# Third sweep of a four-layer graph kernel: the product with the attention weights as seven products of quarters, over pairs of row tiles

## The chip, the cores and the metric

One Trainium2 chip, of which the kernel uses one core. The time is that of one execution on the device, in microseconds (us); the number quoted for a kernel is the median of its runs.

## The reference

Four layers over a graph of 2708 nodes with 512 features, each followed by a residual and a layer norm. `adj` is dense in storage (2708 x 2708). The change lies in layer 1, the attention layer:

```python
h = x @ W_sa
s_left = h @ a_sa[0, :Hd]
s_right = h @ a_sa[0, Hd:]
e = where(adj != 0, exp(-leaky_relu(s_left[:, None] + s_right[None, :], 0.01)), 0)
attn = e / (sum(e, axis=1, keepdims=True) + 1e-05)
x_a = attn @ h
x_b = adj @ (x @ W_gcnb) + b_gcnb
return sigmoid(attn_a * x_a + attn_b * x_b)      # attn_a, attn_b: gates per row
...
x = layernorm(x + layer1(x))
```

The kernel computes `attn @ (x @ W_sa)` as `(e @ x) @ W_sa`, with the row's share `attn_a / (sum(e) + 1e-05)` as a factor behind it.

## The kernel before

The work is a row of seven sweeps over the adjacency matrix; one each for layer 0, the graph convolution and the attention of layer 1, the three hops of layer 2, and layer 3. The change is in the third (index 2, line 1207, `sweep(S[2], RANGES, ...)`).

**Halves and ranges.** The nodes are split into a lower half (h=0) and an upper half (h=1) of 1354 nodes. A sweep takes output columns in ranges: for this sweep (0, 384), (384, 384), (768, 256), (1024, 330), each for both halves at once. With two halves of rows, two of columns and two halves of the features, a range is a product of 2x2 blocks, which the kernel does as seven products P1 to P7 (Strassen's scheme in Winograd's form): s1 to s4 are sums of adjacency blocks, made by VectorE (`comb`, line 411), T1 to T4 sums of feature blocks. Each of P1 to P7 is 10 steps of two 128 x (range's width) matmuls (`step`, line 473), into PSUM banks u, c, d and a, two of each. P1 fills u, P7 c, P5 d; P6 goes on into u, P4 into c, P3 into d, and P2 fills a. Of the eight banks six are so held from P5 to P4.

**Attention weights in this sweep.** Adjacency blocks 11, 21, 22 and 12 are loaded by SP (`load`, line 394). Before a block is used, ScalarE makes `e` from the row of scores (lines 1136 and 1137, a leaky relu and an exponential), and VectorE puts it where the adjacency isn't zero (line 1138). Adjacency tiles, s3 and `e` come from one ring of 38 buffers (`ring_tile`, `trans`), as do sums of finished rows (`d7`).

**What follows a range** (`done2`, line 1158). For each half a range leaves a transposed result C[h, 0..3] of 128 features x width. For each row tile of 128: fetch XB (the gated graph convolution) on SP; multiply with W_sa (`dense`, line 642: eight matmuls of 128x256, W[2] being eight tiles of 128 x 256 in spare parts of the feature tiles); scale with the row's share and add XB on VectorE (line 1170); sigmoid on ScalarE (1173); fetch X1, add, layer norm (1176 to 1179); store X2; transpose on PE and store X2T (1183, 1187); multiply with the last hop's weights W[3] (1191), copy on ScalarE (1193), store Y0. The upper half of a range follows from position 5.15 of its 7 on, the lower half from 7.12 on, in the next range's first positions.

**Order.** Every piece of work is put on a list with a position, in units of one of P1 to P7 (`at`, line 177); `S[2]` is where the third sweep begins. The list, sorted, is the order of priority for a scheduler that places each instruction on its engine when by its own model inputs and buffers are there: an instruction that isn't ready is overtaken by later ones. Those put on the list with `hold` get an extra edge to the instruction before them on their engine (the loop at the end of the program), so they overtake nothing. Each engine then runs its instructions in the order so fixed, waiting where it must.

**Buffers that matter here:** `nat` (6 of 128x512, for fetched tiles and y0), `tmp` (17, for C and rows of scores), `ring` (38), and the eight banks.

**Seven products over pairs of tiles** exist already for the second sweep (`done1`, line 1104 to 1118) and the seventh (`done6`). A pair is the row tile at the same place in both halves. `weight_sums` (655) makes T1 to T4 of the weight's quarters, `row_sums` (666) S1 to S4 of both halves' C, S1 in place and S2 to S4 in six ring tiles; `seven` (680) does six matmuls of 128x256 in a first part and eight in a second, in two banks shared by homes u, c and d, a, and adds what each holds into the output tiles on VectorE, nine times with a scale, with three of the nine behind the first part.

Of the kernel before, what the change touches and what calls it, by code (L numbers as in the profile page):

```python
# [21 lines left out]
F32 = mybir.dt.float32  # L22
BF = mybir.dt.bfloat16
AF = mybir.ActivationFunctionType
ALU = mybir.AluOpType
P = 128
EPS = 1e-5
NH = 1354
KT = 11
# [39 lines left out]
def gnn_kernel(ctx: ExitStack, tc: tile.TileContext, x, adjT, w_sa, a_sa, w_gcn, b_gcn, wab, bab, w_hop, w_out,  # L69
# [76 lines left out]
    def move(queue, dst, src):  # L146

        m = dst.shape[0]
        c = m - m % 16 if m > 16 else m
        queue.dma_start(out=dst[:c], in_=src[:c])  # L150
        if c < m:
            queue.dma_start(out=dst[c:m], in_=src[c:m])

    def ring_tile(nm):
        return pool.tile([P, 384], F32, name=nm, tag="ring", bufs=RING)
# [21 lines left out]
    def at(pos, fn, hold=False):  # L177

        def go():
            n = len(nc.cur_bb.bb.instructions)  # L180
            fn()
            held.update(range(n, len(nc.cur_bb.bb.instructions)))

        events.append((pos, len(events), go if hold else fn))

# [21 lines left out]
    def spare_part(s, g):  # L207

        return groups[s, g][0][:, 2, :]
# [383 lines left out]
    def layernorm(dsts, y, w, on_scalar=False, late=None):  # L593
        st = small.tile([P, 6], F32, name="st")
        nc.vector.bn_stats(st[:w], y[:w])
        mv = small.tile([P, 2], F32, name="mv")
        nc.vector.bn_aggr(mv[:w], st[:w])
        rstd = small.tile([P, 2], F32, name="rstd")
        nc.vector.tensor_scalar(rstd[:w, 0:1], mv[:w, 1:2], EPS, None, ALU.add)  # L599
        nc.gpsimd.tensor_tensor(rstd[:w, 1:2], rstd[:w, 0:1], neg_half[:w], ALU.pow)  # L600
        if on_scalar:
            nc.vector.scalar_tensor_tensor(rstd[:w, 0:1], mv[:w, 0:1], -1.0, rstd[:w, 1:2], ALU.mult, ALU.mult)
        for d, c0, c1 in dsts:
            if on_scalar:
                fn = lambda d=d, c0=c0, c1=c1: nc.scalar.activation(d[:w], y[:w, c0:c1], AF.Identity,
                                                                    bias=rstd[:w, 0:1], scale=rstd[:w, 1:2])
                fn() if late is None else late.append(fn)
                continue
            nc.vector.tensor_scalar(d[:w], y[:w, c0:c1], mv[:w, 0:1], rstd[:w, 1:2], ALU.subtract, ALU.mult)
# [45 lines left out]
    def weight_sums(wq, homes):  # L655

        wt_ = {(f"T{i + 1}", c): homes[2 * i + c] for i in range(4) for c in range(2)}
        sub = lambda o, a, b: nc.vector.tensor_tensor(o, a, b, ALU.subtract)
        for c in range(2):
            sub(wt_["T1", c], wq(0, 1, c), wq(0, 0, c))  # L660
            sub(wt_["T3", c], wq(1, 1, c), wq(0, 1, c))
            sub(wt_["T2", c], wq(1, 1, c), wt_["T1", c])
            sub(wt_["T4", c], wq(1, 0, c), wt_["T2", c])
        return lambda v, c: wt_[v, c] if isinstance(v, str) else wq(*v, c)

    def row_sums(A, n):

        Y = {("A11", c): A[0, c] for c in range(2)}
        Y.update({("A12", c): A[0, 2 + c] for c in range(2)})
        Y.update({("A22", c): A[1, 2 + c] for c in range(2)})  # L670
        for c in range(2):
            for m, a, b, op in (("S3", A[0, c], A[1, c], ALU.subtract), ("S1", A[1, c], A[1, 2 + c], ALU.add),
                                ("S2", None, A[0, c], ALU.subtract), ("S4", A[0, 2 + c], None, ALU.subtract)):
                Y[m, c] = A[1, c] if m == "S1" else ring_tile("d7")
                a = Y["S1", c] if a is None else a
                b = Y["S2", c] if b is None else b
                nc.vector.tensor_tensor(Y[m, c][:, :n], a[:, :n], b[:, :n], op)
        return Y

    def seven(part, Y, wop, H, lo, w, outs, scales, bases):  # L680

        if part == 0:
            x, y = bank("ps_7"), bank("ps_7")
            H.update(u=x[:, :HD], c=x[:, HD:], d=y[:, :HD], a=y[:, HD:])
        for home, a, v in SEV[part]:
            for c in range(2):
                nc.tensor.matmul(H[home][:w], Y[a, c][:, lo : lo + w], wop(v, c),  # L687
                                 start=part == 0 and home in "ud" and c == 0, stop=c == 1, skip_group_check=True)

        def acc(i, e, home, first=False):  # L690
            o = outs[i][:w, e * HD : (e + 1) * HD]
            b = bases[i][:w, e * HD : (e + 1) * HD] if first else o
            if scales is None:
                nc.vector.tensor_tensor(o, H[home][:w], b, ALU.add)
            else:
                nc.vector.scalar_tensor_tensor(o, H[home][:w], scales[i], b, ALU.mult, ALU.add)

        if part == 0 and scales is None:

            nc.scalar.copy(outs[0][:w, :HD], H["u"][:w])  # L700
            nc.scalar.copy(outs[1][:w, HD:], H["c"][:w])
            acc(1, 1, "d")
        elif part == 0:
            acc(0, 0, "u", True)
            acc(1, 1, "c", True)
            acc(1, 1, "d")
        else:
            acc(0, 0, "a")
            for i, e in ((1, 1), (0, 1), (1, 0)):
                acc(i, e, "u", (i, e) != (1, 1))  # L710
            acc(1, 0, "c")
            acc(0, 1, "d")
            for i in range(2) if scales is None else ():
                e = slice(i * HD, (i + 1) * HD)
                nc.vector.tensor_tensor(outs[i][:w, e], outs[i][:w, e], bases[i][:w, e], ALU.add)

    def fetch(src, nm="ld"):
        t = nat(nm)
        move(nc.sync, t[: src.shape[0]], src)
        return t  # L720

    def store_T(dst, xT):
        nc.gpsimd.dma_start(out=dst.rearrange("(c p) i -> p c i", p=P), in_=xT)
# [404 lines left out]

    at(S[2] + 3.2, start2b)

    def prep2(R0, n, h, t, w, a):

        e = trans("e")
        nc.scalar.activation(e[:w, :n], row[R0, h][:w, :n], AF.Prelu, bias=s_right[:w, t : t + 1], alpha=0.01)  # L1136
        nc.scalar.activation(e[:w, :n], e[:w, :n], AF.Exp, scale=-1.0)  # L1137
        nc.vector.scalar_tensor_tensor(a[:w, :n], a[:w, :n], 0.0, e[:w, :n], ALU.not_equal, ALU.mult)  # L1138

    def extra2(pb, r, R0, n, A):  # L1140
# [14 lines left out]
        at(pb + 5.2, lambda: run_sums(R0, n, 0, share))  # L1155
        at(pb + 4.7, lambda: run_sums(R0, n, 1, share))

    def done2(p0, dp, last, R0, n, h, C, tiles):
        gots = []
        for i, (t, lo, w) in enumerate(tiles):  # L1160
            got = {}
            gots.append(got)

            def a(t=t, got=got):
                got["xb"] = fetch(XB[t])

            def b(t=t, lo=lo, w=w, got=got):
                px = dense(lambda c: C[h, c][:, lo : lo + w], W[2], w)
                y = got["xb"]
                nc.vector.scalar_tensor_tensor(y[:w], px[:w], rd[t][:w], y[:w], ALU.mult, ALU.add)  # L1170

            def c(t=t, w=w, got=got):
                nc.scalar.activation(got["xb"][:w], got["xb"][:w], AF.Sigmoid)

            def d(t=t, w=w, got=got):
                got["x1"] = fetch(X1[t])
                y = got["x1"]
                nc.vector.tensor_tensor(y[:w], y[:w], got["xb"][:w], ALU.add)
                layernorm([(y, 0, D)], y, w)
                move(nc.gpsimd, X2[t], y[:w])  # L1180

            def e(lo=lo, w=w, got=got):
                xT = transposed([(got["x1"], 0, D)], w)
                for g, (i0, m) in enumerate(RANGES2):
                    c0, c1 = max(R0 + lo, i0), min(R0 + lo + w, i0 + 2 * m)
                    if c0 < c1:
                        store_T(X2T[g, h][:, c0 - i0 : c1 - i0], xT[:, :, c0 - R0 - lo : c1 - R0 - lo])
                got["xT"] = xT

            def f(t=t, w=w, got=got):  # L1190
                ps = dense(lambda c: got["xT"][:, c, :w], W[3], w)
                o = nat("y0")
                nc.scalar.copy(o[:w], ps[:w])
                move(nc.gpsimd, Y0[t], o[:w])

            m = len(tiles)
            g = min(dp, 0.28)
            p = p0 + g * i
            q = p0 + g * m + 0.02 + 0.04 * i
            at(p - 0.3, a)  # L1200
            at(p, b)
            at(q, c)
            at(q + 0.1, d)
            at(q + 0.32 + 0.6 * dp * i, e)
            at(q + 0.5 + 0.6 * dp * i, f)
# [465 lines left out]
```

## Time and profile before

| | us |
|---|---|
| median of 3 runs | 2844.57 (2844.51 to 2844.64) |
| profiled execution | 2845.67 |
| its span, first to last instruction | 2843.9 |
| PE busy | 2810.6 |
| VectorE busy | 2200.2 |
| ScalarE busy | 541.3 |
| stretch around the third sweep: from before its first product to its last with the attention weights | 785 to 1352 |

The page of the profile gives the share of each engine, then forty slices of the span, the DMA queues, the chain of work that ended last, and the costliest groups of instructions: line, engine, operation, output and inputs by the program's names (buffer numbers left out), count, busy time, mean of one, and what the engine waited for before them. A 128x256 product in 32-bit floats shows as two PE passes. In the third sweep the four ranges' first products begin at about 834, 967, 1110 and 1215 us.

### The profile page before, as it was taken

The page shows a single profiled execution, that of the slowest core. Times are in us where ns is not written, and L with a number is a line of the kernel's source. Part 1 is how long each engine was busy: PE and PEld are TensorE (multiplying, and loading weights), DVE is VectorE, ACT ScalarE, POOL GpSimd, SP SyncE. Part 2 cuts the span into 40 slices and gives each one's busy share as a digit, 9 for nine tenths or more (in the row PEclk, how much of TensorE's full clock was granted, in tenths as well). Part 3 has the DMA queues.
Part 4 walks back from the last instruction along what each step waited for, and adds up shares of the span by engine and source line. Part 5 has one row for each costly group of instructions (what it writes and reads, how often), then busy time and mean ns, then how long its engine had stood idle before and what let it go on. Part 6 is the DMA issues. An engine that isn't in the chain of part 4 may idle for free.

```text
span 2843.9 us, 38510 instructions
## 1 busy us (share of the span) xinstructions
PE 2810.6 (99%) x11486; PEld 1927.0 (68%) x11486; DVE 2200.2 (77%) x5694; ACT 541.3 (19%) x1112; POOL 618.9 (22%) x1114
## 2 busy tenths in 40 slices
PE   7999999999999999999999999999999999999998
PEld 6899765658755656766666666666666666666665
DVE  6999699668736464654699778897888878899987
ACT  4644100101155454540100000000000100100001
POOL 0223232214310101123113033030330211601202
PEclk9999999999999999999999999999999999999999
DMA  7765476436534333564668667566675666854542
GB/s 236 243 193 181 144 229 216 153 126 195 189 92 141 108 116 104 179 193 146 201 207 249 198 208 234 163 210 203 197 234 173 189 194 181 242 167 146 178 141 91
DMA packets 369712, 511.17 MB, mean 180 GB/s; under 512 B 63568, under 2 KB 322884, under 8 KB 369504
## 3 DMA queue, kind: packets, MB, share of 16 engines
q1 hardware_dynamic: 303544, 371.61, 44.3%
q0 software_dynamic: 49376, 126.39, 13.2%
q10 hardware_dynamic: 16584, 10.71, 1.3%
q8 instruction: 91, 1.49, 0.2%
q14 instruction: 117, 0.96, 0.1%
HBM read 424.82 MB, written 83.66 MB: 179 GB/s over the span
## 4 chain that ended last, share of the span: by engine, by line
PE 89%; DVE 6%; issue 2%; DMA 1%; SPq 1%; ACT 1%; POOL 1%; POOLq 0%; DVEq 0%; ACTq 0%
PE accu L1337 12%; PE accd L1337 12%; PE accc L1337 12%; PE accd L484 7%; PE accu L484 7%; PE accc L484 7%; PE ps_d L648 6%; PE acca L1337 6%; PE acca L484 4%; PE accr L1408 2%; PE ps L687 2%; PE accd L470 2%; PE accc L470 2%; PE accu L470 2%; PE acca L470 1%
## 5 line engine op out<-in xcount | busy, mean ns | idle before, releaser
L1282 DVE TENSOR_TENSOR z<-z 128x339 f32<-128x339 f32 (+1 forms) x966 | 455.8, 505 | 11.5 <-PE accu L1337 3.6
L1355 ACT COPY q<-accu 128x338 f32<-128x338 f32 (+1 forms) x84 | 34.6, 444 | 996.1 <-PE accu L1337 896.6
L600 POOL TENSOR_TENSOR rstd<-rstd,neg_half 128x1 f32<-128x1 f32 (+3 forms) x91 | 60.8, 668 | 730.6 <-DVE rstd L599 475.8
L1337 PE MATMUL accc<-s,t 128*128 128x338 f32 (+1 forms) x644 | 198.1, 450 | 0.0
L1337 PE MATMUL accd<-z,t 128*128 128x338 f32 (+1 forms) x644 | 193.9, 448 | 1.4 <-DVE q L1419 1.4
L1337 PE MATMUL accc<-z,t 128*128 128x338 f32 (+1 forms) x644 | 193.5, 448 | 0.6 <-ACT q L1355 0.6
L1337 PE MATMUL accu<-z,t 128*128 128x338 f32 (+1 forms) x644 | 193.8, 448 | 0.0
L1470 POOL DMA_DIRECT2D Y<-y x192 | 105.2, 554 | 364.0 <-DVE y L1465 330.8
L414 DVE TENSOR_TENSOR a<-a,a 128x384 f32<-128x384 f32 (+2 forms) x330 | 163.8, 512 | 23.2 <-PE accu L484 21.7
L1337 PEld LDWEIGHTS accc<-s,t 128*128 128x128 f32 x644 | 120.9, 190 | 64.1 <-issue 7.5
L1337 PEld LDWEIGHTS accc<-z,t 128*128 128x128 f32 x644 | 122.0, 190 | 61.6 <-issue 1.0
L1337 PEld LDWEIGHTS accd<-z,t 128*128 128x128 f32 x644 | 121.9, 190 | 61.2 <-DVE q L1419 2.1
L1337 PEld LDWEIGHTS accu<-z,t 128*128 128x128 f32 x644 | 121.8, 190 | 59.9 <-issue 0.5
L1282 DVE TENSOR_TENSOR s<-z 128x338 f32<-128x338 f32 (+1 forms) x322 | 150.3, 504 | 9.3 <-PE accc L1337 8.0
L1361 DVE TENSOR_TENSOR q<-q,accd 128x338 f32<-128x338 f32 (+1 forms) x112 | 56.2, 502 | 122.3 <-PE accd L1337 122.2
L1138 DVE SCALAR_TENSOR_TENSOR a<-a,e 128x384 f32<-128x384 f32 (+2 forms) x160 | 77.4, 507 | 44.4 <-ACT e L1137 38.6
L1136 ACT ACTIVATE e<-row,s_right 128x384 f32<-128x384 f32 (+5 forms) x176 | 96.4, 569 | 75.1 <-PE accc L484 19.2
L1034 DVE SCALAR_TENSOR_TENSOR mask<-a,mask 128x384 bf16<-128x384 f32 (+2 forms) x152 | 75.9, 506 | 12.5 <-DMA a<-in_adjT 11.2
L417 POOL DMA_DIRECT2D As<-a x120 | 64.9, 545 | 86.9 <-DVE a L414 65.1
L821 DVE SCALAR_TENSOR_TENSOR s<-a,row 128x384 f32<-128x384 f32 (+2 forms) x152 | 75.4, 507 | 7.4 <-ACT row L806 7.4
L1137 ACT ACTIVATE e<-e 128x384 f32<-128x384 f32 (+5 forms) x176 | 79.4, 477 | 1.9
L648 PE MATMUL ps_d<-w,xT 128*128 128x512 f32 (+1 forms) x176 | 79.2, 593 | 0.4 <-ACT xT L639 0.4
(742 smaller groups left out, 5884.8 us busy)
## 6 DMA issues: line engine op xcount, KB each, us to landing
z<-As SPq DMA_DIRECT2D x320, 169.5 KB
z<-As SPq DMA_DIRECT2D x320, 169.0 KB
a<-in_adjT SPq DMA_DIRECT2D x240, 192.0 KB
z<-in_adjT SPq DMA_DIRECT2D x240, 169.5 KB
z<-in_adjT SPq DMA_DIRECT2D x240, 169.0 KB
a<-in_adjT SPq DMA_DIRECT2D x120, 165.0 KB
a<-in_adjT SPq DMA_DIRECT2D x112, 128.0 KB
As<-a POOLq DMA_DIRECT2D x60, 192.0 KB, 3.3
```

Source lines behind the costliest of these rows:

```text
L414: nc.vector.tensor_tensor(A[r, dst, k][:, :n], A[r, a, k][:, :n], A[r, b, k][:, :n], op)
L470: nc.tensor.matmul(B[home, c][:, c0 : c0 + w], a[:, i * P : (i + 1) * P], x[:, d : d + w], start=bool(start and c0 == 0), stop=stop, skip_ ...
L484: nc.tensor.matmul(B[home, c][:, :n], X[STAT[p], k][:, c * P : (c + 1) * P], A[r, MOV[p], k][:, :n], start=bool(start and k == k0), stop=k ...
L648: nc.tensor.matmul(o, lhs(c), r, start=c == 0 and n == 0, stop=c == DC - 1, skip_group_check=True)
L821: nc.vector.scalar_tensor_tensor(t[:w, :n], a[:w, :n], 0.0, row[R0, h][:w, :n], ALU.is_gt, ALU.mult)
L1034: nc.vector.scalar_tensor_tensor(d[:w, :n], a[:w, :n], 0.0, d[:w, :n], ALU.not_equal, ALU.add)
L1136: nc.scalar.activation(e[:w, :n], row[R0, h][:w, :n], AF.Prelu, bias=s_right[:w, t : t + 1], alpha=0.01)
L1137: nc.scalar.activation(e[:w, :n], e[:w, :n], AF.Exp, scale=-1.0)
L1138: nc.vector.scalar_tensor_tensor(a[:w, :n], a[:w, :n], 0.0, e[:w, :n], ALU.not_equal, ALU.mult)
L1282: nc.vector.tensor_tensor(d[:, :n], Z[x + (k,)][:, :n], Z[y + (k,)][:, :n], op)
L1337: nc.tensor.matmul(B[home][:, :n], stat(v, k), a[:, :n], start=bool(start and k == 0), stop=k == nk - 1, skip_group_check=True)
L1470: nc.gpsimd.dma_start(out=rows[:, :, f * P : (f + 1) * P], in_=o[32 * f : 32 * (f + 1), : m * P].rearrange("p (b d) -> p b d", d=P))
```

## The change

In ranges one to three of the third sweep, the product with the attention weights is done for pairs of row tiles, by `seven`, after both halves of the range are there. `row_sums` makes the sums of both halves; `sums2` the sums of W_sa's quarters, with T1 and T2 in spare parts of B21 and B22, T3 in the place of quarter (0, 1) and T4 in the tile `vec`. The last range keeps the plain product, for which `again` loads quarter (0, 1) anew. Pairs follow each other by 1.0 position, from 7.62 of their range; the second part of `seven` comes 0.26 behind the first. `hold` can now be an engine: then only that engine's instructions of the piece are tied to the order of the list. So are the transposes and the product with W[3] of a pair, on PE. The function `node_sums`, which the diff also adds, is called nowhere and left out here.

```diff
--- before
+++ after
@@ -179,7 +179,9 @@
         def go():
             n = len(nc.cur_bb.bb.instructions)
             fn()
-            held.update(range(n, len(nc.cur_bb.bb.instructions)))
+            for i in range(n, len(nc.cur_bb.bb.instructions)):
+                if hold is True or nc.cur_bb.bb.instructions[i].engine == hold.engine:
+                    held.add(i)
 
         events.append((pos, len(events), go if hold else fn))
 
@@ -1128,6 +1130,20 @@
 
     at(S[2] + 3.2, start2b)
 
+    def sums2():
+        v = const.tile([P, D], F32, name="vec", tag="vec")
+        sa = lambda r, e, c: W[2][2 * (2 * r + c) + e]
+        t1, t2 = ([spare_part(s, g) for g in "BD"] for s in ("B21", "B22"))
+        W[9] = weight_sums(sa, t1 + t2 + [sa(0, 1, c) for c in range(2)] + [v[:, :HD], v[:, HD:]])
+
+    def again():
+
+        for c in range(2):
+            nc.scalar.dma_start(out=W[2][2 * c + 1], in_=w_sa[c * P : (c + 1) * P, HD:])
+
+    at(S[2] + 6.4, sums2)
+    at(S[2] + 23.4, again)
+
     def prep2(R0, n, h, t, w, a):
 
 
@@ -1155,11 +1171,77 @@
         at(pb + 5.2, lambda: run_sums(R0, n, 0, share))
         at(pb + 4.7, lambda: run_sums(R0, n, 1, share))
 
...
+    def pairs2(p0, R0, n, C, tiles):
+        Y = {}
+        at(p0 + 0.2, lambda: Y.update(row_sums({(i, c): C[1 - i, c] for i in range(2) for c in range(DC)}, n)))
+        for i, (t0, lo, w) in enumerate(tiles):
+            ts = (t0 + KT, t0)
+            xb, x1, xT, H = [], [], [], {}
+
+            def a(ts=ts, xb=xb):
+                xb.extend(fetch(XB[t]) for t in ts)
+
+            def b(part, ts=ts, lo=lo, w=w, xb=xb, H=H):
+                seven(part, Y, W[9], H, lo, w, xb, [rd[t][:w] for t in ts], xb)
+
+            def c(w=w, xb=xb):
+                for y in xb:
+                    nc.scalar.activation(y[:w], y[:w], AF.Sigmoid)
+
+            def d(ts=ts, x1=x1):
+                x1.extend(fetch(X1[t]) for t in ts)
+
+            def e(j, ts=ts, w=w, xb=xb, x1=x1):
+                y = x1[j]
+                nc.vector.tensor_tensor(y[:w], y[:w], xb[j][:w], ALU.add)
+                layernorm([(y, 0, D)], y, w)
+                move(nc.gpsimd, X2[ts[j]], y[:w])
+
+            def f(j, lo=lo, w=w, x1=x1, xT=xT):
+                v = transposed([(x1[j], 0, D)], w)
+                for g, (i0, m) in enumerate(RANGES2):
+                    c0, c1 = max(R0 + lo, i0), min(R0 + lo + w, i0 + 2 * m)
+                    if c0 < c1:
+                        store_T(X2T[g, 1 - j][:, c0 - i0 : c1 - i0], v[:, :, c0 - R0 - lo : c1 - R0 - lo])
+                xT.append(v)
+
+            def g(j, ts=ts, w=w, xT=xT):
+                ps = dense(lambda c: xT[j][:, c, :w], W[3], w)
+                o = nat("y0")
+                nc.scalar.copy(o[:w], ps[:w])
+                move(nc.gpsimd, Y0[ts[j]], o[:w])
+
+            p = p0 + 0.5 + 1.0 * i
+            at(p - 0.25, a)
+            at(p + 0.15, d)
+            for j in range(2):
+                at(p + 0.26 * j, lambda j=j, b=b: b(j))
+                at(p + 0.45 + 0.02 * j, lambda j=j, e=e: e(j))
+                at(p + 0.84 + 0.06 * j, lambda j=j, f=f: f(j), nc.tensor)
+                at(p + 1.22 + 0.22 * j, lambda j=j, g=g: g(j), nc.tensor)
+            at(p + 0.4, c)
+
     def done2(p0, dp, last, R0, n, h, C, tiles):
-        gots = []
+        if not last:
+            if h == 0:
+                pairs2(p0, R0, n, C, tiles)
+            return
         for i, (t, lo, w) in enumerate(tiles):
             got = {}
-            gots.append(got)
 
             def a(t=t, got=got):
                 got["xb"] = fetch(XB[t])
```

More of the change, by code (lines that the diff above doesn't have):

```diff
@@ L1156, in extra2, with node_sums @@
         at(pb + 4.7, lambda: run_sums(R0, n, 1, share))
+    def node_sums(x, y):
+        Z = {}
+        r = [ring_tile("d7").rearrange("p (c i) -> p c i", i=P)[:, :2, :] for _ in range(4)]
+        a, b = (v[:, i : i + 2, :] for v in (x, y) for i in (0, 2)), None
+        a11, a12, a21, a22 = a
+        for m, o, p, q, op in (("S3", r[0], a11, a21, ALU.subtract), ("S1", r[1], a21, a22, ALU.add),
+                               ("S2", r[2], r[1], a11, ALU.subtract), ("S4", r[3], a12, r[2], ALU.subtract)):
+            nc.vector.tensor_tensor(o, p, q, op)
+            Z.update({(m, c): o[:, c, :] for c in range(2)})
+        for m, o in (("A11", a11), ("A12", a12), ("A22", a22)):
+            Z.update({(m, c): o[:, c, :] for c in range(2)})
+        return Z
```

## The prediction

> **What bounds the kernel now.** The page's head first, then its chain that ended last:
>
> ```profile
> span 2843.9 us, 38510 instructions
> PE 2810.6 (99%) x11486; PEld 1927.0 (68%) x11486; DVE 2200.2 (77%) x5694; ACT 541.3 (19%) x1112; POOL 618.9 (22%) x1114
> ...
> PE 89%; DVE 6%; issue 2%; DMA 1%; SPq 1%; ACT 1%; POOL 1%; POOLq 0%; DVEq 0%; ACTq 0%
> ```
>
> TensorE sets the end. A busy PE may still be waiting inside, so I looked at the third sweep alone, from before its first product to its last with the attention weights (785 to 1352 us), by the windows view, and at whom PE waited for there by the waits view:
>
> ```profile
> 785.00:1352.00 567.00, 566.58 (x2119) 371.30 (x2118) 308.88 (x738) 259.84 (x487) 89.55 (x154) 1.00 0.45 134
> ```
> ```profile
> PE ps_d L648 <- ACT xT L639: 0.4, 1, 0.4
> ```
>
> Columns: window, length, then busy PE, PEld, DVE, ACT, POOL, granted clock, DMA share, GB/s. PE is busy 566.58 of 567 us, and its whole waiting in 780 to 1420 us is one wait of 0.4 us. Nothing is to be had from a shorter wait here, and every matmul taken away is time, if no new wait comes. VectorE is free for 258 us of the 567.
>
> **What goes.** The timeline of PE shows one tile's product with the attention weights, eight lines like these (two lines of eight, and the sweep's next):
>
> ```profile
> 917.72 0.59 PE L648 MATMUL ps_d<-T1B,C 128*128 128x256 f32 x2
> ...
> 920.74 0.59 PE L648 MATMUL ps_d<-T4D,W 128*128 128x256 f32 x2
> 921.17 1.45 PE L484 MATMUL accd<-a,B22A 128*128 128x384 f32 x4
> ```
>
> Each product of 128x256 is two passes (x2). The durations overlap; what counts is start to start: 921.17 - 917.72 = 3.45 us for eight, 0.431 us each. A pair of tiles takes 16, and ranges one to three hold 3 + 3 + 2 = 8 pairs. After the change a pair takes 7 products of quarters, each over two 128-row blocks: 14 of the same form. The same routine runs already in the second sweep, where four products take 555.30 to 557.03 us = 1.73 us, 0.432 each:
>
> ```profile
> 555.30 0.59 PE L687 MATMUL ps<-T4B,d 128*128 128x256 f32 x2
> 555.74 0.59 PE L687 MATMUL ps<-T4D,d 128*128 128x256 f32 x2
> 556.17 0.59 PE L687 MATMUL ps<-T1D,P1c 128*128 128x256 f32 x2
> 556.60 0.59 PE L687 MATMUL ps<-T2D,P1c 128*128 128x256 f32 x2
> 557.03 0.49 PE L484 MATMUL accc<-s,T3D 128*128 128x384 f32 x1
> ```
>
> So PE loses 8 x 2 x 0.431 = **6.90 us**, all of it on the path. Transposes and the product with the hop weights stay as they are, moved only.
>
> **What is added, beside PE.**
> Row sums (L677): 3 ranges x 8, at 0.55 us for 384 columns and 0.42 for 256: 2 x 4.4 + 3.4 = 12.2 us of VectorE. Weight sums: eight of 128x256, like L677's 0.42 form: 3.4 us, once, a range ahead of their use for the second range and just ahead for the first (6.4 against 7.6 in the list). Evacuation: nine of 128x256 with a scale per pair in place of two of 128x512. Rows of the same operation: L696 at 0.475 us, L1170 at 0.75. Per pair 9 x 0.475 - 2 x 0.75 = +2.8 us, for eight +22 us. In all VectorE gets 12.2 + 3.4 + 22 = 38 us more, into 258 free. That cover hides it; where it clusters is a rival below.
> Two reloads of weight quarters (128 KB each) on ScalarE's queue at 23.4, for the last range's plain product at 26.2 and later: nearly three positions, some 50 us, ahead. Behind them on that queue stand only exponentials of the last range, and they wait at most until the second pair of range three has read the old quarters (22.9). Nothing.
> Fetches, sigmoids, layernorms, stores: as many as before, per pair instead of per tile. Those of the lower half (h=1) move about 2.5 positions later, past SP's loads of the next range. The x2 transposes are read by SP at 19.3 and the range that they need has its last at 17.6; y0 is loaded again at 27 and its last is at 24.1. Hidden.
>
> [...]
>
> **Unknown: waits for a bank.** Two banks hold a pair; the second four products add to what VectorE must first have read. The trace has the routine twice. From the view of L687, all its 17 pairs:
>
> ```profile
> its engine sat idle before it (us, times) until:
>   DVE z L696: 6.7, 11
>   DVE y L694: 0.5, 1
> ```
>
> Sweep two (L694, eight pairs, halves 0.26 apart in the list as here): 0.5 us. Last sweep (L696, nine pairs, halves 0.2 apart in a sweep whose positions are shorter): 6.7 us, so 6.0 for eight. From below, the present 0.4 us could vanish. Ends: -0.4 and +6.0. I take 0.5, as the spacing is sweep two's.
>
> **Unknown: the ring.** 38 buffers hold the adjacency tiles, their sums and the exponentials; row sums take six more for two to three positions. The waits view of SP's queue, from the second range's start (966 to 1012 us), shows that they are all in use:
>
> ```profile
> SPq L405 <- PE accc L484: 26.5, 3, 19.0
> SPq L405 <- DVE a L1138: 8.9, 5, 3.1
> ```
>
> Loads of block 22 stop at 966.3 and go on at 993.3, when the first products of P7 (accc, T3) let go of s3 tiles. The row sums will ask in that stretch, and being ahead in the list take the first six of P7's ten releases, 1.29 us apart (two 384-wide products of 0.645): 7.7 us. Pair one then runs in P7 instead of P1. The exponentials for block 22 come 7.7 us later against P7. Now VectorE's last s1 sum ends at 1010.1 and PE reads it at 1026.6 (last of P5, accd T1), 16.5 us of room. P7 keeps about its length (before, three hop products of 3.45; after, up to two pairs at 6.0), so 7.7 fits. From below 0; from above 7.7 in each of the three ranges that follow, 23. I take 0, as in sweep two, whose row sums take the same six: no PE wait at all in 400 to 785 us in the waits view, with VectorE 91% busy where it is fullest:
>
> ```profile
> 558.00:575.00 17.00, 17.00 (x62) 11.06 (x61) 15.44 (x64) 2.17 (x4) 4.81 (x9) 1.00 0.97 330
> ```
>
> Sweep two lacks the exponentials, which need ring tiles and ScalarE too; that is what speaks against the 0.
>
> **Sum.** -6.90 + 0.5 = -6.4 us. The profiled execution took 2845.67 us, its span 2843.9, the median is 2844.57; so I expect 2843.9 - 6.4 = 2837.5 for the span, and for the median 2844.57 - 6.4 = **2838.2 us** (-0.22%). A measurement can tell about 0.2%, 5.7 us, from no change: the forecast is close to that bound, and 0.7 us more of waiting crosses it.
>
> **Rivals.**
> A, *small waits take most of it*. Besides the pair's two banks, six are held by u, c and d from position 2 on, so the transposes and hop products of pairs one and two, now tied to PE's list order, find no free bank until VectorE has emptied a pair; PE takes its instructions in order, so behind a transpose that waits stand the sweep's own products. At 0.75 us per pair (the last sweep's rate) that is 6.0 us, at twice that rate 12. Price: 2837.7 to 2849.7, middle near 2842. For it: eight banks, all named. Against: PE has sweep steps to put in between, which need none.
> B, *the ring starves P5*, slower than before: the six tiles held to position 2.9 leave the exponentials of block 22 four, of which the last block 22 loads keep as many; s1 then comes at the pace of P5's own releases. It decides as soon as the last s1 comes more than 16.5 us later against P5 than now; each range then pays up to 7.7 us, three 23: 2844.57 - 6.9 + 23 = 2860.8; with half, 2849.2. For it: SP's 27 us of blocked queue. Against: sweep two. [...]
> C, *it doesn't do what it says*: the opening of sweep four could wait for loads and swallow the gain. Its loads wait for PE (T3 tiles are freed by the last plain product), so they come forward with it, and PE waits for none at 1340 to 1420 us. About 2844.6.
>
> **How the numbers follow.** Forecast (waits up to 1.2 us) 0.45; A beyond that 0.27, of it about 0.22 within 0.2% and 0.05 slower; B 0.23, with 0.05 in its mildest part within 0.2%; C 0.05, within. Faster by over 0.2% 0.45, within 0.2% 0.32, slower 0.23. Range: from 2837.0 (6.9 and the 0.4 gained, with 0.3 for the medians) to 2853.0, which takes in A whole and the lower half of B and leaves out some 0.13.
>
> **What would show it.** L687 gets 224 passes more (112 products) at 0.216 us, L648 256 fewer. PE idle before L687 and L648 in the third sweep under 1.2 us: forecast. Idle there until VectorE's evacuation or ScalarE's xT and y0 copies: A. Idle at accd<-a,T1 with VectorE's s1 or L1138 as releaser: B. SP should stop longer at P7's releases than 27 us in each range. Wrong altogether if PE's time in 785 to 1352 doesn't fall, or if DMA or another sweep changes.

## The result, and the profile after

The changed kernel takes **2851.85 us** (median of 10 runs, 2850.45 to 2853.24), the kernel before 2844.61 on the same chip (10 runs): a ratio of 1.0024 with an interval of 1.0016 to 1.0033. It is 7.2 us slower where 6.4 us faster was forecast. The time lies inside the range given, on the other side of no change. The profiled execution took 2851.95 us, its span is 2850.1. The page's head and its chain that ended last:

```profile
span 2850.1 us, 38536 instructions
...
PE 2807.8 (99%) x11454; PEld 1920.7 (67%) x11454; DVE 2222.3 (78%) x5782; ACT 531.9 (19%) x1106; POOL 620.1 (22%) x1114
...
PE 87%; DVE 7%; issue 2%; DMA 2%; SPq 1%; POOL 1%; ACT 0%; POOLq 0%; DVEq 0%; ACTq 0%
...
L650 PE MATMUL ps_d<-w,xT 128*128 128x512 f32 (+1 forms) x176 | 80.9, 604 | 4.8 <-DVE ld L698 4.8
```

TensorE has 32 passes fewer, as it should: 8 pairs, two products of two passes each. But the span grew, and the last row is new: PE waits 4.8 us before the product with the hop weights (L648 before, L650 now) for an evacuation by VectorE (L696 before, L698 now). The windows view of the third sweep, then PE's waits from 760 to 1420 us (us in all, times, longest):

```profile
785.00:1352.00 567.00, 556.22 (x2053) 359.01 (x2052) 325.50 (x808) 249.58 (x480) 89.97 (x149) 1.00 0.45 133
```
```profile
PE ps_d L650 <- DVE ld L698: 4.8, 2, 3.3
PE accd L486 <- ACT y L1225: 1.7, 1, 1.7
PE ps_t L639 <- DVE ld L611: 1.7, 3, 0.8
PE ps L689 <- DVE ld L698: 0.8, 1, 0.8
PE ps_t L639 <- ACT xT L641: 0.7, 1, 0.7
PE ps_t L639 <- DVE rstd L601: 0.7, 2, 0.5
```

One wait of 0.4 us has become 10.4 us of waits, while VectorE is busy for 325.5 of the 567 us, 57%.

**A measure for the rest.** A trace of another kernel moves every later position, so I compare stretches: from the start of P3 (the first `accd<-a,B22A`) of one range to the same point in the next. Each of the three stretches that hold pairs should lose 0.862 us per pair: 3, 3 and 2 pairs, so 2.6, 2.6 and 1.7 us. What a stretch lacks of that is waiting. The stretch before them, without pairs, is 118.0 us in all the traces here, and from the end of the third to the last instruction they take 1555.8 to 1557.5 us, with one exception that is named below.

| stretch, us | first | second | third |
|---|---|---|---|
| before | 142.9 | 120.2 | 109.5 |
| forecast without new waits | 140.3 | 117.6 | 107.8 |
| after | 143.1 | 120.9 | 116.8 |
| new waiting | 2.8 | 3.3 | 9.0 |

New waiting comes to 15.1 us. PE's start-to-start distances, less what the same forms take undisturbed, put 2.3, 2.5 and 8.9 us of it into single gaps of over 0.3 us. The third stretch holds the two largest gaps, 1.9 us before 1240.3 and 3.5 us before 1247.2, and behind the second a slower clock. A cut from the timeline with all engines:

```profile
1228.67 0.55 POOL L1327 DMA_DIRECT2D Es<-s  x1
...
1235.28 0.57 ACT L1152 ACTIVATE e<-row,s_right 128x330 f32<-128x330 f32 x1 [5.90 <-DMA Es<-s]
...
1236.28 0.59 PE L689 MATMUL ps<-T4D,d 128*128 128x256 f32 x2
1236.39 0.51 DVE L1154 SCALAR_TENSOR_TENSOR a<-a,e 128x330 f32<-128x330 f32 x1 [5.55 <-ACT e L1153]
...
1243.44 0.87 DVE L698 SCALAR_TENSOR_TENSOR ld<-ps,rd,ld 128x256 f32<-128x256 f32 x2
...
1246.65 0.48 DVE L698 SCALAR_TENSOR_TENSOR ld<-ps,rd,ld 128x256 f32<-128x256 f32 x1
...
1247.19 5.40 PE L650 MATMUL ps_d<-w,xT 128*128 128x512 f32 x8 [3.33 <-DVE ld L698]
```

Read it from the bottom. PE's hop product waits until the last evacuation from a pair's bank is done. PE made that pair's last product at 1236.28, and the evacuation came ten us later. Up to 1236.39 VectorE's queue had stood on `a<-a,e` (L1154), the product that puts the exponentials into an adjacency tile: 5.55 us without work, for ScalarE's exponential, which itself waited 5.90 us for a ring buffer. That buffer held a sum of the extra rows for sweep four, whose store (`Es`) GpSimd had issued at 1228.67; it came free 6.6 us later. From 1236.39 to the first evacuation at 1243.44 VectorE had no pause: seven such products and ten sums of adjacency blocks (L416) were ahead of the evacuations in its queue. So the ten us are the end of a wait and the work that had piled up behind it. The windows view in steps of 5 us (busy PE, PEld, DVE, ACT, POOL, granted clock, DMA share, GB/s):

```profile
1240.00:1245.00 5.00, 3.60 (x12) 2.20 (x12) 5.00 (x13) 4.58 (x12) 0.54 (x1) 1.00 0.74 211
1245.00:1250.00 5.00, 2.81 (x5) 1.31 (x6) 5.00 (x14) 4.39 (x8) 0.52 (x1) 0.86 0.32 102
1250.00:1255.00 5.00, 5.00 (x14) 2.69 (x13) 3.74 (x12) 1.79 (x3) 2.04 (x5) 0.80 0.62 160
```

VectorE is full from 1240 to 1250, and after the 3.33 us wait the granted clock falls, to 0.50 from 1249 to 1252: four 512-wide passes, from 1248.6 to 1251.1, are followed by the next after 0.81 to 0.86 us, not 0.43, which costs 1.6 us more.

In the first two stretches the shape is the same with smaller numbers, and no store holds up the exponential product. In the first it is an adjacency load:

```profile
1004.73 0.87 DVE L698 SCALAR_TENSOR_TENSOR ld<-ps,rd,ld 128x256 f32<-128x256 f32 x2
...
1006.46 0.56 DVE L1154 SCALAR_TENSOR_TENSOR a<-a,e 128x384 f32<-128x384 f32 x1 [0.86 <-DMA a<-in_adjT]
1006.93 0.48 DVE L698 SCALAR_TENSOR_TENSOR ld<-ps,rd,ld 128x256 f32<-128x256 f32 x1
...
1007.47 0.70 PE L689 MATMUL ps<-T3B,W 128*128 128x256 f32 x2 [0.85 <-DVE ld L698]
```

Two of the three evacuations behind a pair's first part are done; VectorE then stands 0.86 us on a product whose adjacency tile is still being loaded, the third evacuation comes behind it, and a product of PE's second part, which needs that bank, waits 0.85 us. In the second stretch VectorE stands for exponentials, 1.23 and 0.57 us, and twice 0.2 us for loads, ahead of six evacuations that PE's next hop product needs:

```profile
1139.12 0.42 DVE L1154 SCALAR_TENSOR_TENSOR a<-a,e 128x256 f32<-128x256 f32 x1 [1.23 <-ACT e L1153]
...
1142.16 2.44 DVE L698 SCALAR_TENSOR_TENSOR ld<-ps,rd,ld 128x256 f32<-128x256 f32 x6
...
1144.27 1.98 PE L650 MATMUL ps_d<-w,xT 128*128 128x512 f32 x4 [1.43 <-DVE ld L698]
```

These two gaps (1.0 and 1.6 us start to start) are 2.6 of the 4.8 us that the first two stretches lose in single gaps. The other 2.2 are four gaps of 0.4 to 0.7 us before transposes (L639), which wait for the layer norm of VectorE and GpSimd.

In SP's queue the pair's fetches stood ahead of the first stretch's loads (its timeline):

```profile
988.77 3.05 SPq L150 DMA_DIRECT2D ld<-XB  x2
993.15 3.84 SPq L150 DMA_DIRECT2D ld<-X  x2
...
1000.27 9.11 SPq L407 DMA_DIRECT2D a<-in_adjT  x8
```

A fetch waits until one of the six `nat` buffers has been stored. In SP's waits from 940 to 1330 us this row was 20.1 us in four waits before, and after it is

```profile
SPq L150 <- DMA Y<-y: 37.0, 7, 10.5
```

### The profile page after: what moved, and what is told of

It is laid out like the page before. It is cut to its first block, busy times and chain, and to the rows that moved or that the text cites. A ratio compares the mean times of both kernels' runs of the same rounds, so it can differ in the third digit from the quotient of the medians.

```text
span 2850.1 us, 38536 instructions
## 1 busy us (share of the span) xinstructions
PE 2807.8 (99%) x11454; PEld 1920.7 (67%) x11454; DVE 2222.3 (78%) x5782; ACT 531.9 (19%) x1106; POOL 620.1 (22%) x1114
## 4 chain that ended last, share of the span: by engine, by line
PE 87%; DVE 7%; issue 2%; DMA 2%; SPq 1%; POOL 1%; ACT 0%; POOLq 0%; DVEq 0%; ACTq 0%
PE accu L1419 12%; PE accd L1419 12%; PE accc L1419 12%; PE accu L486 7%; PE accd L486 6%; PE acca L1419 6%; PE accc L486 6%; PE ps_d L650 4%; PE ps L689 4%; PE acca L486 4%; PE accr L1490 2%; PE accd L472 2%; PE accc L472 2%; PE accu L472 1%; PE acca L472 1%
## 5 line engine op out<-in xcount | busy, mean ns | idle before, releaser
L416 DVE TENSOR_TENSOR a<-a,a 128x384 f32<-128x384 f32 (+2 forms) x330 | 164.9, 514 | 28.8 <-PE accu L486 27.7
L1419 PEld LDWEIGHTS accc<-s,t 128*128 128x128 f32 x644 | 120.9, 190 | 64.0 <-issue 7.5
L1154 DVE SCALAR_TENSOR_TENSOR a<-a,e 128x384 f32<-128x384 f32 (+2 forms) x160 | 77.0, 507 | 29.0 <-ACT e L1153 24.7
L650 PE MATMUL ps_d<-w,xT 128*128 128x512 f32 (+1 forms) x176 | 80.9, 604 | 4.8 <-DVE ld L698 4.8
```

The source lines that it names most:

```text
L416: nc.vector.tensor_tensor(A[r, dst, k][:, :n], A[r, a, k][:, :n], A[r, b, k][:, :n], op)
L650: nc.tensor.matmul(o, lhs(c), r, start=c == 0 and n == 0, stop=c == DC - 1, skip_group_check=True)
L1419: nc.tensor.matmul(B[home][:, :n], stat(v, k), a[:, :n], start=bool(start and k == 0), stop=k == nk - 1, skip_group_check=True)
```

## The experiments

The theories at first:
- **V**, VectorE has too much work where pairs run.
- **R**, the ring is short: the row sums' six tiles keep exponentials waiting (the prediction's rival B).
- **H**, the transposes and hop products, tied to the list's order on PE, stand in front of the sweep's steps.
- **M**, moving the upper half's work behind its range costs, whatever product is used.

Later came:
- **D**, an evacuation stands in VectorE's queue behind an exponential product that has overtaken it and waits for a load or an exponential.
- **P**, the second part of `seven` and what follows come too soon behind the first.
- **S**, SP's fetches hold up the adjacency loads.

All stretches in one table (us; before and after above):

| run | first | second | third | median | ratio to before, interval |
|---|---|---|---|---|---|
| exponentials out of the ring | 148.6 | 125.8 | 116.9 | 2867.21 | 1.0077 (1.0061 to 1.0094) |
| extra rows late | 143.0 | 121.1 | 112.5 | 2849.41 | 1.0011 (1.0001 to 1.0020) |
| no tie on PE | 142.9 | 120.5 | 116.3 | 2854.37 | 1.0031 (1.0020 to 1.0042) |
| pairs with the plain product | 142.9 | 120.2 | 111.1 | 2847.97 | 1.0010 (1.0001 to 1.0019) |
| exponential products tied | 142.0 | 119.3 | 116.8 | 2851.00 | 1.0017 (1.0008 to 1.0027) |
| fetches on GpSimd | 143.0 | 124.6 | 114.9 | 2859.88 | 1.0048 (1.0033 to 1.0063) |
| parts apart | 141.1 | 121.5 | 112.0 | 2846.21 | 1.0000 (0.9990 to 1.0009) |
| parts apart, extra rows late | 141.1 | 120.9 | 107.5 | 2843.55 | 0.9990 (0.9980 to 0.9999) |
| both, and products tied | 140.5 | 117.7 | 107.5 | 2839.38 | 0.9977 (0.9968 to 0.9986) |
| before, extra rows late | 142.9 | 120.2 | 108.9 | 2846.22 | 1.0003 (0.9993 to 1.0012) |
| second part later only | 142.1 | 120.8 | 115.2 | 2851.25 | 1.0019 (1.0010 to 1.0028) |
| followers later only | 149.1 | 124.2 | 113.2 | 2859.05 | 1.0047 (1.0033 to 1.0060) |

The kernel before took 2846.1 to 2846.4 us beside these runs. Stretches come from one profiled execution each, which took between 2.8 us less and 2.3 us more than the run's median.

**Exponentials out of the ring** (R against V):

```diff
-        e = trans("e")
+        e = mask_tile()
```

> The changed kernel with the exponentials of the third sweep out of the ring: kept in the seven 16-bit tiles that this sweep doesn't use (so rounded to 16 bits, which changes the result a little). Theory R (the row sums' six ring tiles starve the exponentials; ScalarE and VectorE run in order, so evacuations of banks queue up behind them): most of the 15 us of new PE waits goes, 2839 to 2842 us, and the last of the three stretches from P3 to P3 falls from 116.8 to about 109. Theory V (VectorE simply has too much work in these stretches): 2850 to 2853, as its work is the same. Theory H (the tie of transposes and hop products to PE's list order): 2849 to 2853.

Slower, by 5.4 and 4.9 us in the first two stretches, where R wanted faster. PE's wait at L689 for L698 went from 0.8 to 9.1 us. A stretch of its timeline:

```profile
1004.51 0.56 DVE L1154 SCALAR_TENSOR_TENSOR r<-r,mask 116x384 f32<-116x384 f32 x1 [1.38 <-DMA r<-in_adjT]
...
1008.65 0.56 DVE L1154 SCALAR_TENSOR_TENSOR r<-r,mask 128x384 f32<-128x384 f32 x1 [3.59 <-DMA r<-in_adjT]
...
1012.11 0.87 DVE L698 SCALAR_TENSOR_TENSOR ld<-ps,rd,ld 128x256 f32<-128x256 f32 x2
...
1013.90 1.22 PE L689 MATMUL ps<-T3B,W 128*128 128x256 f32 x2 [4.58 <-DVE ld L698]
```

What R wanted doesn't come; but with buffers of their own the exponentials may also run further ahead, so the run is no clean test of it. V doesn't fit either: VectorE is idle for 3.59 us just ahead of the evacuations that PE is waiting for. It looks as if products whose exponentials are early pass the evacuations in the order and then stand for the adjacency tile. That suggested D, and is not shown here.

**Extra rows late**: the sums of the extra rows for sweep four, which also take ring tiles, one range later.

```diff
-        for g, p in enumerate((S[2] + 19.3 + 1.1 * i, S[3] + 6.6 + 1.3 * i)):
+        for g, p in enumerate((S[2] + 23.2 + 1.0 * i, S[3] + 6.6 + 1.3 * i)):
```

> The changed kernel with the four pieces of loads and sums for sweep four's extra rows (five ring tiles each) put at positions 23.2 to 26.2 instead of 19.3 to 22.6, behind the pairs of range three. Theory R with the extra rows as the last straw: the third stretch falls from 116.8 to 108 to 110 and the first two stay (143.1, 120.9), 2843 to 2845 us in all. R without them, or V: 2850 to 2853. H: 2850 to 2853.

The third stretch goes from 116.8 to 112.5 us, not to R's 108 to 110, and the others stay. So about half of its new waiting is a meeting of the pairs with the extra rows, which the diff doesn't touch.

**No tie on PE** (H):

```diff
-                at(p + 0.84 + 0.06 * j, lambda j=j, f=f: f(j), nc.tensor)
-                at(p + 1.22 + 0.22 * j, lambda j=j, g=g: g(j), nc.tensor)
+                at(p + 0.84 + 0.06 * j, lambda j=j, f=f: f(j))
+                at(p + 1.22 + 0.22 * j, lambda j=j, g=g: g(j))
```

> The changed kernel without the tie: transposes and hop products of a pair may overtake on PE as all else. H: their waits for VectorE and for banks (8 us by the waits view) go, 2843 to 2846 us. R and V: they stand elsewhere in the order, but the evacuations are as late, 2849 to 2855.

No stretch gains more than 0.5 us, and the median is no lower than after's. H falls.

**Pairs with the plain product** (M): everything moved as in the change, without `sums2`, `again` and `row_sums`.

```diff
-                seven(part, Y, W[9], H, lo, w, xb, [rd[t][:w] for t in ts], xb)
+                px = dense(lambda c: C[1 - part, c][:, lo : lo + w], W[2], w)
+                y, t = xb[part], ts[part]
+                nc.vector.scalar_tensor_tensor(y[:w], px[:w], rd[t][:w], y[:w], ALU.mult, ALU.add)
```

> The order of the changed kernel (both halves of a tile as a pair behind the range, tied as there) with the plain product of 16: no row sums, no weight sums, no reload, two wide evacuations per pair. Theory M (moving the upper half behind the range costs by itself): 2849 us or more. R and V: 2844 to 2846, the waits being gone and PE's work that of before.

The first two stretches are those of before, the third 1.6 us longer. The time lies between what M and the others wanted. The move is nearly free; 13.5 of the 15.1 us, by subtraction, come with the seven products: their row sums, their two parts, their nine evacuations.

**Exponential products tied** (D): on VectorE, block 12's products and those of the last rows keep the list's order, and so overtake no evacuation.

```diff
-                        at(pb + p + f * k / nk, lambda ij=ij, k=k, prepare=prepare: prepare(ij, k))
+                        at(pb + p + f * k / nk, lambda ij=ij, k=k, prepare=prepare: prepare(ij, k), not first and ij == "12" and nc.vector)
...
-                    at(pb + q, lambda h=h, f=rest_prepare: f(h))
+                    at(pb + q, lambda h=h, f=rest_prepare: f(h), not first and nc.vector)
```

> The changed kernel with VectorE's products of the exponentials for block 12 and for the last rows tied to the list's order, so that they can't overtake a pair's evacuations (they are needed at position 4.3 at the earliest). Theory D (evacuations stand in VectorE's order behind products that overtook them and whose load or exponential is late): the waits for evacuations in the first three stretches go, first stretch 143.1 to below 142, 2847 to 2849.5 us in all. Theory V (VectorE has too much work in that time): 2851 to 2853, unchanged. Theory P (the two parts of a pair stand too close): unchanged.

1.1 and 1.6 us less in the first two stretches, nothing in the third. The gap of 1.0 us in the middle of a pair (at 1006 us after) is gone, as is the wait before a hop product in the second (1.6 us at 1142). What stays there are gaps of 0.4 to 0.7 us ahead of transposes. D holds for a part of the first two. The time, 2851.00 us, falls less than D wanted. In the third the two large gaps, 1.9 and 3.5 us, stay as they were, and with them the 5.5 us for which VectorE stands there; overtaking by the products that were tied is not their cause.

**Fetches on GpSimd** (S):

```diff
-                xb.extend(fetch(XB[t]) for t in ts)
+                xb.extend(fetch(XB[t], q=nc.gpsimd) for t in ts)
...
-                x1.extend(fetch(X1[t]) for t in ts)
+                x1.extend(fetch(X1[t], q=nc.gpsimd) for t in ts)
```

> The changed kernel with the pairs' fetches on GpSimd's queue instead of SP's, where they wait for a buffer with the loads of block 12 and the last rows behind them. Theory S (a form of D: those loads are late because of the fetches ahead of them): 2846 to 2849.5 us, the first stretch below 142. V and P: 2851 to 2853. If a fetch that waits blocks GpSimd's layer norm steps: slower, up to 2860.

Slower, 124.6 us in the second stretch. GpSimd also makes a step of the layer norm (`rstd`) and issues the stores that free the `nat` buffers, and those now stand behind fetches that wait for such a buffer (two waits of 165.1 us together). The blocked queue was moved, not removed. SP's row of waits for a fetch's buffer falls from 37.0 to 12.9 us, yet VectorE still stands 0.72 us for a load at the same place in the first stretch and PE 0.70 us behind it; so S gets no support, though it isn't disproved. Here is the exception: 1561.2 us behind the third stretch, 4 to 5 more than in the other traces. They don't lie in any sweep. PE runs behind the changed kernel's times by the same 3.0 us from the third stretch to its last product, ScalarE's last step ends at 2850.16 us, and the span ends 8.2 us later, against 3.0 to 3.4 us in the other traces. A drain of GpSimd, from 2848.71 on, takes 8.43 us, against 3.7 to 4.0 in the others. So of the 8 us that this run is slower than the changed kernel, some 5 are at the program's end; GpSimd's queue carries 32 issues more (1048 for 1016), and why the drain is longer with them isn't shown.

**Parts apart** (P): second part 0.45 behind the first, in place of 0.26, and what follows it later by as much.

```diff
-                at(p + 0.26 * j, lambda j=j, b=b: b(j))
-                at(p + 0.45 + 0.02 * j, lambda j=j, e=e: e(j))
-                at(p + 0.84 + 0.06 * j, lambda j=j, f=f: f(j), nc.tensor)
-                at(p + 1.22 + 0.22 * j, lambda j=j, g=g: g(j), nc.tensor)
-            at(p + 0.4, c)
+                at(p + 0.45 * j, lambda j=j, b=b: b(j))
+                at(p + 0.64 + 0.02 * j, lambda j=j, e=e: e(j))
+                at(p + 1.03 + 0.06 * j, lambda j=j, f=f: f(j), nc.tensor)
+                at(p + 1.41 + 0.22 * j, lambda j=j, g=g: g(j), nc.tensor)
+            at(p + 0.5900000000000001, c)
```

> The changed kernel with the second part of a pair 0.45 instead of 0.26 positions behind the first, and all that follows it 0.19 later. Theory P (the second part comes before VectorE has emptied the first): the waits of the second part and of the hop products fall, 2846 to 2849 us. D and V: 2850 to 2853, as the order on VectorE is what is late.

2.1 us less in the first stretch, 4.8 in the third, in the second 0.6 more. Time equal to before's: spacing alone returns some 6 us of the 15.

**Parts apart and extra rows late**, both edits as above:

> The run before with the extra rows' loads and sums at 23.2 to 26.2 as well. If the two gains add (the extra rows' ring tiles gave 2.4 to 4.3 us in their run): 2842 to 2846 us. If they are one and the same wait: 2846 to 2849.

2843.55 us, where the two gains were to add. The third stretch falls to 107.5 us: its whole waiting is gone, and 0.3 us that it had before. The second keeps 120.9, with one wait of 2.5 us before a transpose (at 1144), for L698.

**Both, and the products tied**, all three edits:

> The parts 0.45 apart and what follows 0.19 later, the extra rows' loads late, and VectorE's products of block 12 tied to the list's order, all three. If the three causes are separate: the stretches 140.2 to 141, 119 to 119.5 and 107.5 to 108, which sum to some 5 us under before's; 2840 to 2842 us against 2845 to 2846.5 of before on this chip. If tie and distance remove the same wait: as with two of them, 2843 to 2844.5.

140.5, 117.7 and 107.5 us: less than before by 2.4, 2.6 and 2.1 us, 7.0 in all (from unrounded times), and the time is under the 2840 to 2842 us expected. PE's waits from 760 to 1420 us are an empty list. Its page and its window:

```profile
span 2837.3 us, 38557 instructions
...
PE 2803.7 (99%) x11454; PEld 1921.0 (68%) x11454; DVE 2220.7 (78%) x5782; ACT 533.5 (19%) x1106; POOL 617.5 (22%) x1114
```
```profile
785.00:1352.00 567.00, 567.00 (x2116) 369.94 (x2115) 334.60 (x831) 254.33 (x485) 94.63 (x162) 1.00 0.48 139
```

This is V's end, and that of R for the row sums, which keep their six ring tiles here. VectorE runs the same 5782 instructions as in the changed kernel and has more work in the window, 334.6 us against 325.5 (the sweep ends earlier, so more of what follows falls into it), and PE is busy for all of its 567 us. Only the order differs. In its timeline the evacuations now come in time, and VectorE waits for PE:

```profile
1001.91 1.46 DVE L698 SCALAR_TENSOR_TENSOR ld<-ps,rd,ld 128x256 f32<-128x256 f32 x3
...
1010.53 1.74 DVE L698 SCALAR_TENSOR_TENSOR ld<-ps,rd,ld 128x256 f32<-128x256 f32 x4 [3.33 <-PE ps L689]
```

At 2839.38 us (11 runs, 2838.33 to 2840.32) it beats both kernels; before took 2846.11 beside it.

**Before, extra rows late**, to see whether that edit is a gain by itself:

> The kernel before with the extra rows' loads late, a control: if what they cost is their place in the ring beside the row sums, nothing changes here (stretches 142.9, 120.2, 109.5, within 0.5 us). If they cost something of themselves: the last stretch falls by 1 us or more.

0.7 us in the third stretch, between the two expectations, and none in the time. So of the 4.3 us that the edit returns to the changed kernel, some 3.6 are left, by subtraction, for a collision that the change made.

**Second part later only** and **followers later only**, the two halves of "parts apart":

> The changed kernel with only the second parts (and sigmoid and layer norm behind them) 0.19 later, transposes and hop products where they were. If it is the second part that comes before VectorE has emptied the first: the gain of the run with all of it later, 2846 to 2848 us, third stretch about 112. If it is transposes and hop products that come before their inputs: 2850 to 2853.

> The changed kernel with only the transposes and hop products 0.19 later and the parts 0.26 apart as they were. The other half of the same question: 2846 to 2848 us if these come too early, 2850 to 2853 if it is the second parts.

The first alone returns 1.1, 0.1 and 1.6 us. The second alone costs 5.9 and 3.3 us in the first two stretches and returns 3.6 in the third; its time, 2859.05 us, is outside both expectations. Only together do they give 2.1 and 4.8. The timeline of the second shows what its delay runs into:

```profile
1010.46 1.08 DVE L1154 SCALAR_TENSOR_TENSOR a<-a,e 128x384 f32<-128x384 f32 x2 [6.47 <-DMA a<-in_adjT]
...
1013.80 2.44 DVE L698 SCALAR_TENSOR_TENSOR ld<-ps,rd,ld 128x256 f32<-128x256 f32 x6
...
1015.89 1.33 PE L639 MATMUL ps_t<-ident,ld 128*128 128x128 f32 x5 [5.63 <-DVE ld L698]
```

The same picture as D's, larger than anywhere: VectorE stands 6.47 us for a load, six evacuations are behind it, and PE, through with the second part early, waits 5.63 us before a transpose.

## Why the prediction was wrong

**PE's saving: right.** 6.90 us were forecast. In the run without waits PE's busy time over the span is 2803.7 us against 2810.6, 6.9 less, and its stretches are 7.0 us shorter than before's (0.7 of that in the third comes to the kernel before too, with its extra rows late).

**The waits for a bank: the step that failed.** I took 0.5 us from the second sweep and had 6.0 as the upper end. The runs show 15.1, less the 1.6 that the move alone costs. The second sweep has the same routine at the same spacing, and VectorE's queue stands there too, as the trace of the kernel before shows in the middle of a pair:

```profile
547.85 0.56 DVE L1034 SCALAR_TENSOR_TENSOR mask<-a,mask 128x384 bf16<-128x384 f32 x1 [3.82 <-DMA a<-in_adjT]
...
552.71 0.75 DVE L694 TENSOR_TENSOR y<-ps,y 128x256 f32<-128x256 f32 x2
...
554.44 1.03 PE L687 MATMUL ps<-w,C 128*128 128x256 f32 x4
```

VectorE waits 3.82 us for a load and the last evacuations come at 552.71; PE, which asks for these banks only with the next pair at 554.44, waits for nothing. Two things differ in the third sweep. Of the three homes that the first part fills, ScalarE empties two in the second sweep (lines 700 and 701, a copy) and VectorE one; in the third VectorE empties all three, with a scale. And behind a pair PE has transposes and hop products, which need a bank, or VectorE's result, within a few us (a hop product began 2.4 us after a pair's last product at 1010.16, and PE asked for a bank 2.8 us after the one at 1140.08). I took over the rate without them; which of the two weighs more wasn't told apart by a run. In VectorE's queue of the third sweep stand the exponential products, and each of them may wait for a load (0.86 us after; 6.47 with the followers later) or for an exponential (5.55). The evacuations behind come late by such a wait and by the work that it has piled up, and PE's order has a pair's second part, its transposes and its hop products tied to them.

**The ring: 0 was wrong in the third stretch alone.** One exponential waited 5.90 us for a ring buffer there, held not by the row sums whose six tiles I had counted but by an extra-row sum until its store was through. The sign that I had named, SP stopping longer than 27 us at P7's releases, isn't there: from 966 to 1012 us SP waits 7.4 us for them after, against 26.5 before. Rival B named the resource, but its site (s1 late before P5's `accd<-a,T1`) doesn't appear: the 1.7 us wait at that step is for ScalarE's copy of y0, which stood in ScalarE's queue behind the exponential that waited for the ring. In the first two stretches ScalarE waits up to 9.5 us (at 1094.8) for a buffer that a product of VectorE frees, but just as long in the run without waits of PE (at 1093.7); the ring isn't what costs there.

**VectorE's cover: the size was over, the conclusion from it wrong.** I had 38 us more in 258 free. The single durations were right: 72 evacuations at 0.477 us for sixteen at 0.75 are 22 us more, as forecast. But the page shows only 22.1 more in all in the span (2222.3 against 2200.2), as the busy time counts the overlap of neighbours once: six evacuations in a row take 2.44 us and start 0.39 apart, less than the 0.475 that the prediction took for one. And free time in a sum over 567 us says nothing of when a given instruction is reached: with the followers later VectorE was idle for 6.47 us up to 1010.46, though PE had begun that pair's last product at 1007.73, and its six evacuations began at 1013.80.

**Moved fetches: "hidden" was half right.** The move (of the upper half, h=1, which the prediction calls the lower) costs 0, 0 and 1.6 us. SP's waits for a fetch's buffer rose from 20.1 to 37.0 us, and adjacency loads stand behind them; that D's products wait because of it isn't shown.

**The clock.** No term of the forecast's sum stands for a lower clock. After the 3.33 us wait the granted clock was 0.86 and 0.80 in the two windows of 5 us, and 0.50 from 1249 to 1252; the four passes that are followed by the next after 0.81 to 0.86 us, not 0.43, cost 1.6 us. What sets it is not shown: the last section has a wait of 3.33 us after which it stayed at 1.00.

**The rivals.** A had the right place (PE idle until VectorE's evacuation) with a top price of 12 us, B a part of the cause in one stretch and the right size. I kept them apart, each with its own price. In the run they were one chain: load, exponential or, in one stretch, ring, then exponential product, evacuation, bank. That the range takes in the time is B's doing, whose lower half set the upper end, and no merit of the sum.

**Open.** In the third stretch the extra rows bring ring tiles and 16 sums on VectorE, which were not told apart. A larger ring wasn't tried. S wasn't isolated. Why GpSimd's drain is longer with the fetches on its queue isn't known. How the new waiting divides between tie, spacing and extra rows is known only as far as the runs above add up. Why the scheduler's own model puts an exponential product ahead of an evacuation wasn't looked into.

## What to carry to other kernels

Before a change that adds evacuations, look at what else stands in the same engine's queue and what each of those waits for: in the third stretch the first evacuation of the late banks came 7 us after a wait of 5.55 us had ended, behind the 17 instructions that had piled up, with VectorE busy for 57% of the sweep's window. A wait rate measured in one stage did not hold in another: 0.5 us became 13.5, where VectorE empties all three homes of the first part and transposes and hop products follow a pair by 2.4 to 2.8 us. So before taking a rate over, compare who empties the banks and how far off their next user is; which of the two weighed more here wasn't shown. And where a change of 0.2% loses, try its spacing: with the work unchanged, three moves in the order turned +7.2 us into -6.7.

## What the runs showed of the hardware that was not expected

In the changed kernel the exponential that waited for a ring buffer under a store (`Es`) began at 1235.28, 6.6 us after the store was issued at 1228.67, twelve times the 0.55 us that the issue shows on GpSimd.

The granted clock after a wait of TensorE was not the same in all of them. After 4.58 us (exponentials out of the ring) the granted clock was 0.50 from 1014 to 1018 us, and after 5.63 us (followers later) 0.50 from 1016 to 1020. With the fetches on GpSimd a gap of 3.1 us start to start (2.9 idle) was followed by 0.57 from 1147 to 1151, while in the same trace a gap of 3.5 us at 1247 (3.33 idle) was followed by 1.00 up to 1259. Of these two the shorter was the one with the lower clock behind it; what decides it is not shown.

GpSimd's last drain took 8.43 us in the run with 32 more issues on its queue and 3.7 to 4.0 us in all others; it ends behind the last work of every other engine.
